# Graph convolution on one core: sums of moving node blocks pass through DRAM to 49 fixed blocks

## The chip, the cores and the metric

The kernel runs on one core of a Trainium2 chip. The metric is the device time of one execution in microseconds, the median of several runs. TensorE appears in the profile as PE (its weight loads as PEld), VectorE as DVE, ScalarE as ACT, GpSimd as POOL, and the queue that issues the plain DMAs as SP.

## The reference

There are N = 6250 nodes with D = 512 features in float32 and E = 100000 edges, sorted by their target `dst`. With h the rectified layer norm of x, and norm = -dinv[src] * dinv[dst], where dinv is one over the root of a node's count as a source:

```
prop(h) = segment_sum(h[src] * norm, dst)            # 6250 x 512
h  = relu(layernorm(x))
h1 = leaky(layer_norm(h @ W1_0 + prop(h) @ W1_1 + b1) * gamma + beta)
out = x + h1 @ W2_0 + prop(h1) @ W2_1 + b2
```

So each of two layers gathers 100000 rows of 2 KB by `src`, sums them by `dst`, and multiplies two 6250 x 512 matrices by two 512 x 512 weights.

## The kernel before

A setup of some 124 us loads x into the tile `places`, counts the sources, and makes `dinv`, the layer norm's scales and the table `tab[0]` of rows h * dinv that the first layer gathers. The second layer gathers from `tab[1]`, which the first layer writes, and reads its own rows back from `h_tab`.

The edges lie in 782 chunks of 128. `gather` (L400) is one indirect DMA on POOL: 128 rows of 2 KB into one of 57 slots of `places`, the slots being used in a ring. A gather waits until PE has done with the slot's earlier chunk.

The nodes are worked on in moving blocks. `block_plan` cuts the edges at every 1888th edge into BL = 53 blocks; block b starts at the node where edge 1888 b lies, read from `dst` at run time, so each block's edges lie in chunks that are known when the program is built, while its first node is known only at run time. On the mean a block owns 118 nodes and not 128, and its rows in x, h_tab, tab[1] and out are addressed through a register on SP (`row[b]`). 15 new chunks are needed by a block, and about 24 pairs of chunk and quarter of a block are multiplied.

PE, POOL and SP follow the order of the program, which is written by hand; ACT and DVE are ordered by the scheduler. For block b, in each layer, the program has:

- gathers up to 57 chunks past the block's first one (`gather_to`);
- `load(b + 2)`: SP loads `xt` (L474), and `scales` (L477, first layer) or `h` (L479, second layer);
- `own(b + 1)`: four transposes of h on PE (L460), copied to `hT` by ACT (L488);
- `sums(b)`: DVE compares edge targets with the block's nodes (`sel`, L507), PE multiplies `sel` into the gathered rows (L517, 32 columns of the array at a time, so four products at once), ACT copies the result to `agg`, scaled by the nodes' -dinv (L520);
- half of block b + 1's own products (`start_products`, L495, 4 PE instructions), four transposes of `agg` (L460), a copy to `aT` on DVE (L603), the other half of L495, and the products of `aT` with the other weight (L609, 8 PE instructions);
- `finish`: DVE and ACT do bias and layer norm (first layer) or bias and residual (second), and SP stores to `tab[1]` and `h_tab` (L546, L550) or to `out` (L529).

A count of the edges that were seen, and checks on the block starts, decide at the end whether a slow general path runs as well.

Of the kernel before, what the change touches and what calls it, by code (L numbers as in the profile page):

```python
# [19 lines left out]
P = 128  # L20
# [7 lines left out]
RAW = 60  # L28
SPREAD = 3.2
# [35 lines left out]
def gnn_kernel(  # L65
# [34 lines left out]

    nc = tc.nc
# [24 lines left out]
    scales = dram.tile([3, NB * P], F32, name="scales")  # L126

# [10 lines left out]
    signs = const.tile([P, 2], F32, name="signs")  # L138
# [6 lines left out]
    sb = const.tile([P, BL, 3], F32, name="sb")  # L145
    sn = const.tile([P, BL, 2], F32, name="sn")
# [84 lines left out]
    nc.gpsimd.memset(signs[:, 0:1], -1.0)  # L231
    nc.gpsimd.memset(signs[:, 1:2], SLOPE)
# [18 lines left out]
    all3 = ep.tile([P, 3, NB], F32, name="all3")  # L251
# [4 lines left out]
    for (i0, n), t in zip(groups, xs):  # L256
        n = min(n, NB - LAST - i0)
        for j in range(n):
            junk = ep.tile([P, D], BF, name="junk", bufs=2)
            nc.scalar.activation(junk, t[:, j, :], AF.Copy, accum_out=sums[:, i0 + j : i0 + j + 1])  # L260
        nc.scalar.activation(nm_all[:, i0 : i0 + n], sums[:, i0 : i0 + n], AF.Copy, scale=-1.0 / D)
        for j in range(n):
            junk = ep.tile([P, D], BF, name="junk", bufs=2)
            nc.scalar.activation(junk, t[:, j, :], AF.Square, bias=nm_all[:, i0 + j : i0 + j + 1],
                                 accum_out=sq_all[:, i0 + j : i0 + j + 1])
# [42 lines left out]
    with tc.tile_pool(name="fold", bufs=1) as dp, tc.tile_pool(  # L308
        name="fold_ps", bufs=1, space=bass.MemoryType.PSUM
    ) as dps:  # L310
        deg = dps.tile([P, NB], F32, name="deg")
        each = ident.rearrange("k (n s) -> k s n", s=2)
        for t in range(2):
            for i in range(2):
                nc.tensor.matmul(deg[t * LO : (t + 1) * LO, :], each[:, i, :], both[:, :, t, i],
                                 start=(i == 0), stop=(i == 1))
        root = dp.tile([P, NB], F32, name="root")
        some = dp.tile([P, NB], F32, name="some")
        nc.vector.tensor_scalar_max(root, deg, 1.0)
        nc.scalar.activation(root, root, AF.Sqrt)  # L320
        nc.vector.tensor_single_scalar(some, deg, 0.0, op=OP.is_gt)
        nc.vector.reciprocal(root, root)
        nc.vector.tensor_mul(dinv, root, some)
        nc.vector.tensor_scalar_mul(ndinv, dinv, -1.0)
        nc.vector.tensor_copy(all3[:, 2, :], dinv)

        nc.vector.tensor_mul(sc[:, 0, :], rs_all, dinv)
        nc.vector.tensor_mul(sc[:, 1, :], nb_all, dinv)
# [20 lines left out]
    odd = ep.tile([1, 2, BL], F32, name="odd")  # L349
# [10 lines left out]
    with tc.tile_pool(name="scales_ps", bufs=1, space=bass.MemoryType.PSUM) as fps:  # L360
        all_ps = fps.tile([NB, 3, P], F32, name="all_ps")
        for k in range(3):
            nc.tensor.transpose(all_ps[:, k, :], all3[:, k, :], ident)
        all_sb = ep.tile([NB, 3, P], F32, name="all_sb")
        nc.scalar.activation(all_sb, all_ps, AF.Copy)
        nc.sync.dma_start(scales.rearrange("k (b p) -> b k p", p=P), all_sb)

# [4 lines left out]
    n_unseen = nc.values_load(unseen[0:1, 0:1], min_val=0, max_val=2 * BL,  # L372
# [6 lines left out]
def usual_path(tc, have):  # L379
    nc = tc.nc  # L380
    (x, out, tab, h_tab, scales, sidx, dl, iota_r, w_sb, W2_1, W2_0, w_late, ident, eps, ones, first_i, first, owned,
     astray, signs, sb, sn, bias1, bias2, gam, bet, n_seen, unseen, ranges, NK, N, E, D, NB, BL, NC, KD, places,
     order, groups, xs, sc, pick, src_lo, src_hi, p_id) = (
        have[n] for n in ("x out tab h_tab scales sidx dl iota_r w_sb W2_1 W2_0 w_late ident eps ones first_i first "
                          "owned astray signs sb sn bias1 bias2 gam bet n_seen unseen ranges NK N E D NB BL NC KD "
                          "places order groups xs sc pick src_lo src_hi p_id").split())
    AHEAD = 2
    R = len(order)
    with ExitStack() as es:
# [3 lines left out]
        row = {}  # L393
# [24 lines left out]
        def find(tag, bufs):  # L418
# [7 lines left out]
            is_lo.append(pool.tile([P, 4, P], F32, name="is_lo"))  # L426
# [3 lines left out]
        def look_up(tag, bufs):  # L430
# [4 lines left out]
            at = looked  # L435
            assert at + 4 <= gathered
# [5 lines left out]
            nc.vector.tensor_tensor(is_hi, src_hi[:, at : at + 4, None].to_broadcast([P, 4, NB]),  # L442
# [6 lines left out]
            for j in range(4):  # L449
                nc.scalar.activation(zr(at + j), zr(at + j), AF.Relu, bias=ac[:, j, 1:2], scale=ac[:, j, 0:1])  # L450
# [13 lines left out]
        def load(layer, b):  # L464

            if b % LOADED == 0:
# [4 lines left out]
                for k in range(n):  # L471
                    row[b + k] = bass.ds(vals[k], P)
            xt = pool.tile([P, D], F32, name="xt", bufs=AHEAD + 1)
            nc.sync.dma_start(xt, x[row[b], :])  # L474
            h = pool.tile([P, D], F32, name="h", bufs=AHEAD + 1)
            if layer == 0:
                nc.sync.dma_start(sb[:, b, :], scales[:, row[b]].rearrange("k p -> p k"))  # L477
            else:
                nc.sync.dma_start(h, h_tab[row[b], :])  # L479
            return xt, h  # L480

        def own(layer, b, xt, h):

            if layer == 0:
                nc.vector.tensor_tensor(sn[:, b, :], sb[:, b, 2:3].to_broadcast([P, 2]), signs, op=OP.mult)
                nc.scalar.activation(h, xt, AF.Relu, bias=sb[:, b, 1:2], scale=sb[:, b, 0:1])
            ps, hT = transposed(h, "hT")
            nc.scalar.activation(hT, ps, AF.Copy)  # L488
            if layer == 1 and b == BL - 1:
                nc.vector.tensor_add(xt, xt, bias2)  # L490
            return hT

        def start_products(u_ps, hT, w0, kcs):
            for kc in kcs:
                nc.tensor.matmul(u_ps, hT[:, kc, :], w0[:, kc, :], start=(kc == 0), stop=False)  # L495

        def sums(layer, b):
            rng = ranges[b]
            at = [sum(hi - lo for lo, hi in rng[:q]) for q in range(NQ + 1)]
# [5 lines left out]
            for q, (lo, hi) in enumerate(rng):  # L505
                wide = [P, hi - lo, Q]
                nc.vector.tensor_tensor(sel[:, at[q] : at[q + 1], :], dl[:, lo:hi, None].to_broadcast(wide),  # L507
                                        node[:, None, q * Q : (q + 1) * Q].to_broadcast(wide), op=OP.is_equal)
            if layer == 0:
                held = pool.tile([P, NK, Q], BF, name="held", bufs=1)  # L510
                nc.scalar.activation(held[:, : at[NQ], :], sel[:, : at[NQ], :], AF.Copy,
                                     accum_out=n_seen[:, b : b + 1])
            ps = psum.tile([P, D], F32, name="ps")
            for s in range(max(hi - lo for lo, hi in rng)):
                for q, (lo, hi) in enumerate(rng):
                    if lo + s < hi:
                        nc.tensor.matmul(ps[q * Q : (q + 1) * Q, :], sel[:, at[q] + s, :], zr(lo + s),  # L517
                                         start=(s == 0), stop=(lo + s == hi - 1))
            agg = pool.tile([P, D], F32, name="agg", bufs=1)
            nc.scalar.activation(agg, ps, AF.Copy, scale=sn[:, b, 0:1])  # L520
            return agg

        def finish(layer, b, v, xt):
            if layer == 1:
                o = pool.tile([P, D], F32, name="t")
                if b < BL - 1:
                    nc.vector.tensor_add(v, v, bias2)  # L527
                nc.vector.tensor_add(o, v, xt)
                nc.sync.dma_start(out[row[b], :], o)  # L529
# [14 lines left out]
            nc.scalar.activation(t, v, AF.Copy, scale=sn[:, b, 1:2])  # L544
            nc.vector.scalar_tensor_tensor(t, v, sb[:, b, 2:3], t, op0=OP.mult, op1=OP.max)
            nc.sync.dma_start(tab[1][row[b], :], t)  # L546
# [3 lines left out]
            nc.sync.dma_start(h_tab[row[b], :], g)  # L550
# [6 lines left out]

        ACT = mybir.EngineType.Activation
# [3 lines left out]
        held = [load(0, b) for b in range(AHEAD)]  # L562
# [4 lines left out]
        for layer in range(2):  # L567
            w0, w1 = (w_late[:, 1], w_late[:, 0]) if layer else (w_sb[1], w_sb[0])
            if layer == 1:
                gathered = 0  # L570
                held = [load(layer, b) for b in range(AHEAD)]
            for b in range(BL):
# [7 lines left out]
                if b == 0:  # L580
                    hT = own(layer, 0, *held[0])
# [5 lines left out]
                if b + AHEAD < BL:  # L587
                    held.append(load(layer, b + AHEAD))
                if b + 1 < BL:
                    hT = own(layer, b + 1, *held[b + 1])  # L590
# [3 lines left out]
                agg = sums(layer, b)  # L594
# [4 lines left out]
                if b + 1 < BL:  # L599
                    next_ps = psum.tile([P, D], F32, name="u_ps")  # L600
                    start_products(next_ps, hT, w0, range(KD // 2))
                aT_ps, aT = transposed(agg, "aT")
                nc.vector.tensor_copy(aT, aT_ps)  # L603
                if b + 1 < BL:
                    start_products(next_ps, hT, w0, range(KD // 2, KD))
                if layer == 0:
                    another()
                for kc in range(KD):
                    nc.tensor.matmul(u_ps, aT[:, kc, :], w1[:, kc, :], start=False, stop=(kc == KD - 1))  # L609
# [5 lines left out]
                finish(layer, b, u_ps, held[b][0])  # L615
                u_ps = next_ps
# [329 lines left out]
```

## Time and profile before

| | |
|---|---|
| median of 7 runs | 2693.85 us (2684.55 to 2718.3) |
| the profiled execution | 2683.43 us, its span 2681.6 us |
| busy: PE, DVE, ACT, POOL | 71%, 25%, 18%, 56% of the span |
| DMA | 527.33 MB, mean 197 GB/s |
| gathers | 1504 of 0.95 us each, and 60 from x itself |
| first layer | from about 124 us to 1421 us of the span |
| second layer | from 1421 us to the end |

An instruction's row in the profile has its start, its duration and, in brackets, how long its engine had been idle before it and what ended that; "remote" stands for a release that the profile cannot put down to an instruction. Ends of PE's instructions are modelled.

### The profile page before, as it was taken

How to read it: one execution, taken by the hardware profiler on the slowest of the kernel's cores; microseconds unless marked ns; L12 is line 12 of the kernel's file. 1: busy time of each engine (PE TensorE's matmuls, PEld its weight loads, DVE VectorE, ACT ScalarE, POOL GpSimd, SP SyncE). 2: the span in 40 equal slices, each digit the busy share in tenths (PEclk: the TensorE clock that was granted, in tenths of full speed). 3: DMA queues.
4: the chain of work that ended last, by engine and by line, in shares of the span. 5: the costliest groups of instructions: out<-in, count | busy, mean ns of one | idle time of the engine just before them, and what ended most of it. 6: DMA issues, size and time to landing. Idle time of an engine off the chain costs nothing.

```text
span 2681.6 us, 23467 instructions
## 1 busy us (share of the span) xinstructions
PE 1906.7 (71%) x8137; PEld 731.6 (27%) x8137; DVE 681.8 (25%) x1422; ACT 471.7 (18%) x924; POOL 1502.8 (56%) x1579
## 2 busy tenths in 40 slices
PE   4627768777777876776683378777777677786878
PEld 4413223222222222222231123222222222222323
DVE  8923323322322332232240111111111111111111
ACT  8723212222211221121120000000000000000000
POOL 4254565666655665565516566655665565666560
PEclk9757889888988988888896688888988798897989
DMA  9474666767657765665626576766676666766672
GB/s 319 173 252 141 197 202 198 216 204 215 200 176 229 212 201 170 195 204 182 185 92 197 161 215 208 219 192 187 211 216 187 201 209 195 219 207 206 189 213 72
DMA packets 209696, 527.33 MB, mean 197 GB/s; under 512 B 51850, under 2 KB 53559, under 8 KB 209566
## 3 DMA queue, kind: packets, MB, share of 16 engines
q0 software_dynamic: 125120, 410.09, 52.2%
q1 hardware_dynamic: 84446, 115.63, 12.4%
q8 instruction: 66, 1.08, 0.2%
q14 instruction: 64, 0.52, 0.1%
HBM read 471.00 MB, written 54.60 MB: 196 GB/s over the span
## 4 chain that ended last, share of the span: by engine, by line
PE 40%; another core or an unknown queue 30%; issue 14%; DVE 11%; ACT 3%; DMA 0%; POOL 0%; SPq 0%; ACTq 0%; DVEq 0%; POOLq 0%
PE u_ps L609 17%; PE ps L517 15%; PE u_ps L495 6%; DVE sel L507 2%; DVE aT L603 1%; PE aT_ps L460 1%; PE hT_ps L460 1%; DVE lo L285 1%; DVE hi L285 1%; DVE g L549 1%; DVE u_ps L541 1%; DVE u_ps L539 1%; DVE node L504 1%; DVE u_ps L531 1%
## 5 line engine op out<-in xcount | busy, mean ns | idle before, releaser
L400 POOL DMA_INDIRECT places<-tab,sidx x1504 | 1426.9, 949 | 1029.0 <-PE ps L517 425.7
L517 PE MATMUL ps<-places,sel 128*32 128x512 f32 x4984 | 786.2, 620 | 129.3 <-issue 116.8
L517 PEld LDWEIGHTS ps<-places,sel 128*32 128x32 f32 x4984 | 197.8, 112 | 628.5 <-issue 607.0
L609 PE MATMUL u_ps<-places,aT 128*128 128x512 f32 x424 | 253.9, 754 | 141.1 <-DVE aT L603 114.7
L507 DVE TENSOR_TENSOR sel<-dl,node 128x192 f32<-128x192 f32 (+3 forms) x424 | 122.7, 346 | 777.0 <-remote 482.2
L495 PE MATMUL u_ps<-w,hT 128*128 128x512 f32 x424 | 244.4, 706 | 100.5 <-issue 87.8
L609 PE MATMUL u_ps<-w,aT 128*128 128x512 f32 x424 | 240.9, 721 | 94.5 <-DVE aT L603 89.8
L495 PE MATMUL u_ps<-places,hT 128*128 128x512 f32 x424 | 227.9, 663 | 7.5 <-issue 7.5
L488 ACT ACTIVATE hT<-hT_ps 128x512 f32<-128x512 f32 x106 | 63.2, 596 | 940.3 <-PE hT_ps L460 607.3
L520 ACT ACTIVATE agg<-ps,sn 128x512 f32<-128x512 f32 x106 | 72.9, 687 | 783.9 <-remote 463.9
L460 PE MATMUL aT_ps<-ident,agg 128*128 128x128 f32 x424 | 74.1, 302 | 153.4 <-ACT agg L520 85.3
L609 PEld LDWEIGHTS u_ps<-places,aT 128*128 128x128 f32 x424 | 100.0, 245 | 299.6 <-issue 155.1
L603 DVE COPY aT<-aT_ps 128x512 f32<-128x512 f32 x106 | 73.3, 692 | 425.5 <-remote 321.8
L609 PEld LDWEIGHTS u_ps<-w,aT 128*128 128x128 f32 x424 | 96.8, 234 | 230.3 <-issue 123.8
L495 PEld LDWEIGHTS u_ps<-w,hT 128*128 128x128 f32 x424 | 85.4, 224 | 216.6 <-issue 195.2
L460 PEld LDWEIGHTS aT_ps<-ident,agg 128*128 128x128 f32 x424 | 55.4, 156 | 236.9 <-issue 126.3
L527 DVE TENSOR_TENSOR u_ps<-u_ps,bias 128x512 f32<-128x512 f32 x52 | 36.4, 700 | 305.1 <-PE u_ps L609 153.0
L495 PEld LDWEIGHTS u_ps<-places,hT 128*128 128x128 f32 x424 | 78.8, 206 | 115.7 <-issue 115.7
L460 PE MATMUL hT_ps<-ident,h 128*128 128x128 f32 x424 | 65.8, 279 | 58.6 <-DVE is_lo L427 29.2
L531 DVE TENSOR_TENSOR u_ps<-u_ps,bias 128x512 f32<-128x512 f32 x53 | 37.1, 700 | 258.5 <-PE u_ps L609 171.1
L400 POOL DMA_INDIRECT places<-in_x_dram,sidx x44 | 44.1, 1003 | 81.1 <-ACT places L413 55.1
L460 PEld LDWEIGHTS hT_ps<-ident,h 128*128 128x128 f32 x424 | 53.7, 144 | 115.2 <-issue 90.5
(117 smaller groups left out, 986.7 us busy)
## 6 DMA issues: line engine op xcount, KB each, us to landing
xt<-in_x_dram SPq DMA_DIRECT2D x106, 256.0 KB
places<-tab,sidx POOLq DMA_INDIRECT x1504
tab<-t SPq DMA_DIRECT2D x53, 256.0 KB
h_tab<-g SPq DMA_DIRECT2D x53, 256.0 KB
h<-h_tab SPq DMA_DIRECT2D x53, 256.0 KB
out_dram<-t SPq DMA_DIRECT2D x53, 256.0 KB
places<-in_x_dram SPq DMA_DIRECT2D x4, 1792.0 KB
tab<-places SPq DMA_DIRECT2D x4, 1792.0 KB
```

The lines of the kernel that those rows point to most:

```text
L285: nc.vector.tensor_tensor(t, s[:, g * 2 * GJ : (g + 1) * 2 * GJ].rearrange("p (j s) -> p j s", s=2)[:, :, None, :] .to_broadcast([EP, GJ, ...
L400: nc.gpsimd.indirect_dma_start(out=zr(t), out_offset=None, in_=x if layer == 0 and t < RAW else tab[layer], in_offset=bass.IndirectOffsetO ...
L460: nc.tensor.transpose(ps[:, kc, :], h[:, kc * P : (kc + 1) * P], ident)
L488: nc.scalar.activation(hT, ps, AF.Copy)
L495: nc.tensor.matmul(u_ps, hT[:, kc, :], w0[:, kc, :], start=(kc == 0), stop=False)
L507: nc.vector.tensor_tensor(sel[:, at[q] : at[q + 1], :], dl[:, lo:hi, None].to_broadcast(wide), node[:, None, q * Q : (q + 1) * Q].to_broad ...
L517: nc.tensor.matmul(ps[q * Q : (q + 1) * Q, :], sel[:, at[q] + s, :], zr(lo + s), start=(s == 0), stop=(lo + s == hi - 1))
L520: nc.scalar.activation(agg, ps, AF.Copy, scale=sn[:, b, 0:1])
L527: nc.vector.tensor_add(v, v, bias2)
L531: nc.vector.tensor_add(v, v, bias1)
L603: nc.vector.tensor_copy(aT, aT_ps)
L609: nc.tensor.matmul(u_ps, aT[:, kc, :], w1[:, kc, :], start=False, stop=(kc == KD - 1))
```

## The change

The moving blocks stay for the sums alone. ACT copies block b's sums to `agg` unscaled, and SP writes them to a new DRAM table `sum_d` at the block's rows (register address). Behind that stand NB = 49 fixed blocks of 128 nodes (the last one starts at N - 128). `need[i]` is the moving block after which all rows of fixed block i are there, if block starts are off from their even spacing by at most `DRIFT` = 32 nodes, which a new term of the check tests. After the write of block need[i], SP reads rows of `sum_d` into `prop[i]`, and ACT scales them by `ndinv`. `dense(i)` then does what followed the sums before: own transposes, both products and `finish`, for fixed block i, one moving block later than its read. In each layer the moving blocks 0, 1, 10, 23, 36 and 49 (of 0 to 52) are followed by the next block's sums with no `dense` between; all others are followed by one `dense`, and before the sums of block 52 stand two more, of fixed blocks 46 and 47, whose rows block 51 completes. The last fixed block is the last moving block too, and takes its sums without DRAM.

Own rows (`h`, `xt`), `tab[1]`, `h_tab` and `out` have fixed addresses, and scales come from tiles of the setup, so the first layer's loads of `scales` go. `own(i + 1)` stood before `sums` and now stands in `dense`, after the sums. One more pass over the node rows' scales (`last3`) is read back in the setup.

```diff
         def sums(layer, b):
...
-            agg = pool.tile([P, D], F32, name="agg", bufs=1)
-            nc.scalar.activation(agg, ps, AF.Copy, scale=sn[:, b, 0:1])
-            return agg
+            agg = pool.tile([P, D], F32, name="agg")
+            if b == BL - 1:
+                nc.scalar.activation(agg, ps, AF.Copy, scale=last_nd)
+                prop[NB - 1] = agg
+                return
+            nc.scalar.activation(agg, ps, AF.Copy)
+            nc.sync.dma_start(sum_d[row(b), :], agg)
+            for i in range(NB):
+                if need[i] == b:
+                    prop[i] = pool.tile([P, D], F32, name="prop")
+                    nc.sync.dma_start(prop[i], sum_d[at[i] : at[i] + P, :])
+                    nc.scalar.activation(prop[i], prop[i], AF.Copy, scale=ndinv[:, i : i + 1])
...
+        def dense(layer, i, u_ps, w0, w1):
+            if layer == 1:
+                own_x[i] = pool.tile([P, D], F32, name="xt")
+                nc.sync.dma_start(own_x[i], x[at[i] : at[i] + P, :])
+                if i == NB - 1:
+                    nc.vector.tensor_add(own_x[i], own_x[i], bias2)
+            if i + AHEAD < NB:
+                load(layer, i + AHEAD)
+            next_ps = None
+            if i + 1 < NB:
+                hT = own(layer, i + 1)
+                next_ps = psum.tile([P, D], F32, name="u_ps")
+                start_products(next_ps, hT, w0, range(KD // 2))
+            aT_ps, aT = transposed(prop.pop(i), "aT")
+            nc.vector.tensor_copy(aT, aT_ps)
+            if i + 1 < NB:
+                start_products(next_ps, hT, w0, range(KD // 2, KD))
+            for kc in range(KD):
+                nc.tensor.matmul(u_ps, aT[:, kc, :], w1[:, kc, :], start=False, stop=(kc == KD - 1))
+            finish(layer, i, u_ps)
+            return next_ps
...
-                if b + AHEAD < BL:
-                    held.append(load(layer, b + AHEAD))
-                if b + 1 < BL:
-                    hT = own(layer, b + 1, *held[b + 1])
...
-                agg = sums(layer, b)
+                if b == BL - 1:
+                    while need[i] < b:
+                        u_ps = dense(layer, i, u_ps, w0, w1)
+                        i += 1
+                sums(layer, b)
...
+                while i < NB and need[i] < b + (b == BL - 1):
+                    u_ps = dense(layer, i, u_ps, w0, w1)
+                    i += 1
```

Counts for both layers together: sums 106 as before; `dense` passes 98 for 106; 104 writes of 256 KB to `sum_d` and 96 reads; 294 other block loads and stores of 256 KB for 318.

## The prediction

> **What bounds the kernel now.** I read the busy times first, then the list of waits, then the timeline of three stretches: the blocks at the very end, a block in the middle of the second layer, and that layer's start. The span of the profiled execution is 2681.6 us and its time 2683.4; the median of the runs is 2693.85, so I add 10.4 at the end. A difference of 0.5%, 13.5 us, is about what a measurement of this kernel can tell from none.
>
> ```profile
> PE 1906.7 (71%) x8137; PEld 731.6 (27%) x8137; DVE 681.8 (25%) x1422; ACT 471.7 (18%) x924; POOL 1502.8 (56%) x1579
> L400 POOL DMA_INDIRECT places<-tab,sidx x1504 | 1426.9, 949 | 1029.0 <-PE ps L517 425.7
> ```
>
> A gather takes 0.95 us and 0.30 to the next, so the 15 of a block take 18.75 us and the 782 of a layer 978 us. Between the sums of blocks 0 and 49 of the second layer (their `agg` at 1509.19 and 2627.01) lie 49 periods of 22.8 us. POOL is therefore not the bound by itself: it waits 425.7 us for PE to free slots.
>
> Now the waits on PE's results:
>
> ```profile
> ACT agg L520 <- remote: 463.9, 64, 74.1
> POOL places L400 <- PE ps L517: 425.7, 152, 15.0
> DVE aT L603 <- remote: 321.8, 49, 10.6
> PE u_ps L609 <- DVE aT L603: 204.5, 49, 6.9
> ```
>
> The two handoffs from PE that carry a block, `agg` and `aT`, are late in about half of the blocks without a releaser that the profile can name. The last two blocks of the program, whose gathers are all done, show the chain without this:
>
> ```profile
> 2640.07 1.98 PE L495 MATMUL u_ps<-places,hT 128*128 128x512 f32 x4
> 2640.25 0.69 ACT L520 ACTIVATE agg<-ps,sn 128x512 f32<-128x512 f32 x1 [5.55 <-PE ps L517]
> 2641.89 0.60 PE L460 MATMUL aT_ps<-ident,agg 128*128 128x128 f32 x4
> 2642.33 1.88 PE L495 MATMUL u_ps<-places,hT 128*128 128x512 f32 x4
> 2642.53 0.69 DVE L603 COPY aT<-aT_ps 128x512 f32<-128x512 f32 x1 [1.12 <-PE aT_ps L460]
> 2644.05 3.60 PE L609 MATMUL u_ps<-places,aT 128*128 128x512 f32 x8
> 2647.48 0.60 PE L460 MATMUL hT_ps<-ident,h 128*128 128x128 f32 x4
> 2648.01 6.21 PE L517 MATMUL ps<-places,sel 128*32 128x512 f32 x46
> ```
>
> From one `agg` (2640.25) to the next (2654.32) there are 14.07 us: 6.2 of sums and 7.9 of everything else on PE. PE never stands still, since half of L495 lies over each handoff. The block at 1900 us, with gathers going, looks different:
>
> ```profile
> 1900.79 0.69 ACT L520 ACTIVATE agg<-ps,sn 128x512 f32<-128x512 f32 x1 [7.71 <-remote]
> ...
> 1908.51 0.69 DVE L603 COPY aT<-aT_ps 128x512 f32<-128x512 f32 x1 [6.17 <-remote]
> ...
> 1909.25 5.83 PE L609 MATMUL u_ps<-places,aT 128*128 128x512 f32 x8 [5.35 <-DVE aT L603]
> ```
>
> The transposes for this `aT` stand at 1901.53 to 1902.19, the copy at 1908.51. PE has idled 5.35 us by then, and its next eight products take 5.83 us and not 3.60, at half the clock. Over all blocks `agg` begins 2.3 us after the last row of the sums (0.1 in the last four blocks) and `aT` 2.3 us late in the first layer and 3.6 in the second (0.04 without gathers). All long cases lie where POOL has issued gathers without a pause for some 7 us or more. The strongest case is the second layer's start, where 57 empty slots let POOL run without a pause:
>
> ```profile
> 1438.76 6.19 PE L517 MATMUL ps<-places,sel 128*32 128x512 f32 x34 [3.40 <-DMA places<-tab,sidx]
> ...
> 1496.57 0.95 POOL L400 DMA_INDIRECT places<-tab,sidx  x1 [0.30 <-issue]
> 1505.82 0.95 POOL L400 DMA_INDIRECT places<-tab,sidx  x1 [8.30 <-remote]
> 1509.19 0.69 ACT L520 ACTIVATE agg<-ps,sn 128x512 f32<-128x512 f32 x1 [74.13 <-remote]
> ```
>
> Sums that PE had by 1448 are handed over at 1509, after the run of gathers. So the bound is PE's chain of handoffs, stretched from 14.1 us a block to 22.8 by POOL's gathers.
>
> **The change, part by part**, on the profiled 2683.4 us.
>
> *Eight passes fewer* (four in each layer) of L495, L460, L609 and `finish`. Their cost at most is a period less its sums, 22.8 - 6.1 = 16.7 us each, 134 in all. At least it is nothing, for the gathers of those blocks remain. The nearest row is the layer's start: where PE frees many slots at once, POOL runs on end, and PE's handoffs stand until it ends. Two sums in a row free 30 slots, which is half of that run. So I credit what a period has beyond its own 15 gathers, 22.8 - 18.75 = 4.05 us each: **-32** (-134 to 0).
>
> *A hop moves behind the sums.* `own(i + 1)` stood before the sums, and ACT's copy of `hT` (0.60 us) lay beside them. Now PE transposes h behind the sums and stands until ACT has made `agg` (0.69, ahead of `hT` in ACT's order) and `hT`. Before, it went on at once with half of L495. Without gathers, the last sums to the end of the `aT` transposes takes 2642.49 - 2640.14 = 2.35 us. After: 0.1 to `agg`, 0.69, 0.04, 0.60 and 0.05 make 1.5, then half of L495 (1.72 without its overlap) and 0.6 for the transposes, 3.8. The transposes of h no longer stand ahead of the sums, 0.53. That is 3.8 - 2.35 - 0.53 = 0.95 for each of 96 passes: **+92** (0, if late handoffs cover it, to 92).
>
> *The late handoff loses its cover.* `agg` is late by over 1 us in 64 of 106 blocks, and 1.9 us of L495 stood over it. Only the 0.6 of the transposes do now, since ACT works `agg` off first, and `hT` stands behind it. All of that is 1.3 x 64 = 83, and for 98 passes in place of 106, 75. But a gather run ends when it ends, and a late `hT` makes `aT` less late. I take a third: **+25** (0 to 75).
>
> The clock enters here. After 5.35 us without work the eight of L609 took 5.83 us for 3.60; the new stop of 1.5 us is far from that. [...]
>
> *The way through DRAM.* SP writes `sum_d`, waits for the landing, reads `prop`, and ACT scales it (0.69). At the second layer's start POOL was released 2.92 us after the store to `tab[1]` was issued (1418.39 to 1421.31), and PE's transposes came 4.56 us after the issue of the load of h (1421.88 to 1426.44). The trip is then 0.69 + 2.9 + 4.6 + 0.69, about 9 us, against 22.8 to the pass that needs it. Where two sums stand on end, at four places of each layer, another 6.1 us of sums is the least cover: up to 3 us each, 23. ACT's scale stands in ACT's order ahead of `hT` and the next `agg`, so a late trip would stop these, and PE with them; SP's loads of h and `xt` queue behind the read, two blocks ahead of need. I take **0** (0 to 23). [...]
>
> *The layers' ends.* Pass 47 needs block 51, which pass 45, 46's products and the trip's 9 us overlap: **0** (0 to 18, both trips bare).
>
> *Scales.* In the first layer ACT waited 77.9 us in 24 pieces for loads of `scales`, which go. PE itself waited 9.9 us for ACT's `h`: **-10** (-78 to 0).
>
> *Bytes.* 104 writes and 96 reads of 256 KB less 24 loads: 46 MB on 527, 9%. At 197 GB/s that would be 234 us if the path were the bound; but gathers land 3.3 us after issue and are issued two blocks ahead, and PE waits 6.6 us for them in all. **0** (0 to 60, which is a quarter of that).
>
> *The rest.* Setup's extra read **+3**; 96 scales on ACT (18% busy), SP's issues and DVE's unchanged work 0, under the sums.
>
> Sum: -32 + 92 + 25 + 0 + 0 - 10 + 0 + 3 = +78; 2683.4 + 78 + 10.4 = **2772 us**.
>
> **The rivals.** *Fewer passes pay in full.* If the new hop falls into lateness that the gathers set anyway, and POOL's 33 tiles of lead carry the double sums, the gain is up to 134: -134 - 10 + 3, 2552 us; with 4 us a pass it is 2655. I put it at 2610. For it: 8 x 16.7 is the largest term here, and POOL waits on PE. Against it: the 57-gather run, where lead did not help. It decides if the hop costs under 1.4 us a pass (134 / 96). *Nothing moves*: gain and hop cancel, 2694. *The trip stands in the way*: `prop`'s wait holds ACT ahead of each `agg`. With a trip at 9 us it can't, but at over 22.8 it does; 2.5 us at each pass would be +240, about 2930. Against it: the 2.92 and 4.56 us rows, taken beside a busy DMA. *The general path runs*, if block starts drift by over 32 nodes: these edges drift by 18 at most, so it is nearly excluded.
>
> **How the numbers follow.** The forecast gets 0.59, full pay 0.25, no change 0.10, the trip 0.05, the general path 0.01. That makes faster 0.25, same 0.10, slower 0.65. The forecast's own range is 2710 to 2880: the hop half covered at one end, lateness uncovered and 40 us of bytes and trips at the other. Down to the other case's middle it is 2605 to 2880, with a tenth left out on either side.
>
> **What would show it.** In the profile after: PE's first half of the own products (now L496) waiting for ACT's `hT` behind each sums, about 1.5 us in the blocks without gathers, where `agg` to `agg` should be 15.0 for 14.07; about 23.7 with gathers; ACT's `agg` still released by "remote"; no waits on `scales`; about 573 MB; and next to no wait of the scaling of `prop` (L541) on DMA, but for the double sums. I am wrong if the period with gathers stays at or under 22.8 (then the hop is covered), if two sums in a row cost no longer run of late handoffs, or if L541 waits at most blocks.

## The result

The changed kernel takes 2867.99 us (median of 20 runs, 2845.34 to 2893.11) against 2696.5 of the kernel before (52 runs); the ratio is 1.0709, with an interval of 1.0677 to 1.0741. It is slower, as forecast, and inside the range, but the forecast of +78 us was less than half of it: 7.09% of 2693.85 are +191. Below, one hundredth of a ratio is taken as 27 us. Beside two of the runs below, e17 and m4, the kernel before itself took 2090.8 us, so these two are compared with that value alone.

The changed kernel's busy times and its gathers, from its page:

```profile
PE 1886.4 (66%) x7945; PEld 736.7 (26%) x7945; DVE 650.0 (23%) x1328; ACT 516.0 (18%) x996; POOL 1499.9 (53%) x1577
...
L414 POOL DMA_INDIRECT places<-tab,sidx x1504 | 1426.3, 948 | 1171.3 <-PE ps L528 579.5
```

PE has 192 products and transposes fewer and 20 us less work, and the span is 162 us longer. POOL's gathers cost what they did; POOL waits 154 us longer for PE to free slots (579.5 for 425.7). So PE stands more. Its list of waits (total, number, longest) says at what:

```profile
ACT agg L535 <- remote: 763.9, 57, 85.1
...
DVE aT L593 <- remote: 569.4, 53, 12.6
...
PE u_ps L496 <- ACT hT L491: 293.6, 61, 13.2
...
ACT prop L541 <- DMA prop<-sum_d: 242.7, 47, 10.1
...
PE u_ps L597 <- DVE aT L593: 183.1, 55, 6.5
```

The third line is new: the products of the own rows (L496, which was L495) wait for the copy `hT`. So is the fourth: ACT waits 47 times, 5.2 us on the mean, for the read of `sum_d`. One block of the second layer in the timeline (start, duration, idle time before and its releaser):

```profile
1915.13 0.66 PE L474 MATMUL hT_ps<-ident,h 128*128 128x128 f32 x4
...
1917.49 0.60 ACT L535 ACTIVATE agg<-ps 128x512 f32<-128x512 f32 x1 [15.43 <-remote]
...
1920.41 0.60 ACT L491 ACTIVATE hT<-hT_ps 128x512 f32<-128x512 f32 x1 [2.33 <-remote]
...
1921.07 3.78 PE L496 MATMUL u_ps<-places,hT 128*128 128x512 f32 x4 [5.27 <-ACT hT L491]
...
1930.93 0.69 DVE L593 COPY aT<-aT_ps 128x512 f32<-128x512 f32 x1 [11.87 <-remote]
1931.68 5.40 PE L597 MATMUL u_ps<-places,aT 128*128 128x512 f32 x8 [4.18 <-DVE aT L593]
```

The transposes of h end at 1915.79, and ACT copies them at 1920.41, although it was free from 1918.09. PE stands 5.27 us, and its next four products take 3.78 us where four took 1.98 without gathers; the granted clock is 0.50 over these 3.78 us, and 0.82 over the whole span (0.86 before). The handoff of `aT` is late all the same: the transposes of `prop` end at 1925.70, and DVE copies them at 1930.93. At the end of the layer, without gathers, the same place looks as it was priced:

```profile
2780.99 0.66 PE L474 MATMUL hT_ps<-ident,h 128*128 128x128 f32 x4
...
2782.33 0.58 ACT L491 ACTIVATE hT<-hT_ps 128x512 f32<-128x512 f32 x1
2782.96 1.98 PE L496 MATMUL u_ps<-places,hT 128*128 128x512 f32 x4 [1.31 <-ACT hT L491]
```

From the starts of the sums in both traces: a moving block of the second layer, blocks 3 to 50, takes 25.15 us for 22.78 before. As only 43 of these 47 have a pass, that is 27.5 a pass. The first layer's go from 23.59 to 23.76. From block 50 to the last sums the two layers take 70.7 and 55.6 us where they took 35.3 and 33.9.

### The profile page after: what moved, and what is told of

Same layout as the page of the kernel before. It is cut to its first block, busy times and chain, and to the rows that moved or that the text cites. A ratio compares the mean times of both kernels' runs of the same rounds, so it can differ in the third digit from the quotient of the medians.

```text
span 2843.4 us, 22620 instructions
## 1 busy us (share of the span) xinstructions
PE 1886.4 (66%) x7945; PEld 736.7 (26%) x7945; DVE 650.0 (23%) x1328; ACT 516.0 (18%) x996; POOL 1499.9 (53%) x1577
## 4 chain that ended last, share of the span: by engine, by line
another core or an unknown queue 34%; PE 32%; issue 15%; DVE 12%; DMA 3%; ACT 3%; SPq 1%; POOL 1%; ACTq 0%; DVEq 0%; POOLq 0%
PE u_ps L597 12%; PE ps L528 11%; PE u_ps L496 6%; DVE sel L518 2%; DVE aT L593 1%; DMA sum_d<-agg 1%; PE aT_ps L474 1%; PE hT_ps L474 1%; DMA prop<-sum_d 1%; DVE hi L287 1%; DVE t L548 1%; DVE node L515 1%; DVE g L569 1%; DVE st L554 1%
## 5 line engine op out<-in xcount | busy, mean ns | idle before, releaser
L414 POOL DMA_INDIRECT places<-tab,sidx x1504 | 1426.3, 948 | 1171.3 <-PE ps L528 579.5
L528 PE MATMUL ps<-places,sel 128*32 128x512 f32 x4984 | 746.2, 609 | 123.6 <-issue 100.6
L496 PE MATMUL u_ps<-w,hT 128*128 128x512 f32 x392 | 271.8, 831 | 253.1 <-ACT hT L491 141.7
L496 PE MATMUL u_ps<-places,hT 128*128 128x512 f32 x392 | 266.9, 818 | 241.7 <-ACT hT L491 151.9
L597 PE MATMUL u_ps<-places,aT 128*128 128x512 f32 x392 | 216.6, 704 | 120.6 <-DVE aT L593 113.9
L535 ACT ACTIVATE agg<-ps 128x512 f32<-128x512 f32 x104 | 62.1, 597 | 1157.4 <-remote 763.9
L597 PE MATMUL u_ps<-w,aT 128*128 128x512 f32 x392 | 203.0, 666 | 71.8 <-DVE aT L593 69.2
L496 PEld LDWEIGHTS u_ps<-w,hT 128*128 128x128 f32 x392 | 95.0, 269 | 343.0 <-issue 176.6
L496 PEld LDWEIGHTS u_ps<-places,hT 128*128 128x128 f32 x392 | 92.6, 262 | 327.9 <-issue 163.1
L541 ACT ACTIVATE prop<-prop,ndinv 128x512 f32<-128x512 f32 x96 | 69.2, 720 | 513.0 <-issue 270.4
L597 PEld LDWEIGHTS u_ps<-places,aT 128*128 128x128 f32 x392 | 84.9, 225 | 248.4 <-DVE aT L593 140.7
L597 PEld LDWEIGHTS u_ps<-w,aT 128*128 128x128 f32 x392 | 81.5, 214 | 188.4 <-issue 100.1
L474 PEld LDWEIGHTS aT_ps<-ident,prop 128*128 128x128 f32 x384 | 73.4, 202 | 96.3 <-issue 95.1
L474 PE MATMUL aT_ps<-ident,prop 128*128 128x128 f32 x384 | 85.0, 364 | 0.1
```

The costliest lines, as they stand in the source:

```text
L414: nc.gpsimd.indirect_dma_start(out=zr(t), out_offset=None, in_=x if layer == 0 and t < RAW else tab[layer], in_offset=bass.IndirectOffsetO ...
L474: nc.tensor.transpose(ps[:, kc, :], h[:, kc * P : (kc + 1) * P], ident)
L528: nc.tensor.matmul(ps[q * Q : (q + 1) * Q, :], sel[:, cols[q] + s, :], zr(lo + s), start=(s == 0), stop=(lo + s == hi - 1))
L535: nc.scalar.activation(agg, ps, AF.Copy)
L541: nc.scalar.activation(prop[i], prop[i], AF.Copy, scale=ndinv[:, i : i + 1])
```

## The experiments

**The hop, undone and alone.** e1 puts the own transposes of the next fixed block ahead of the sums again; e2 moves them behind the sums in the kernel before.

```diff
# e1, in the changed kernel
+                early = own(layer, i + 1) if b < BL - 1 and need[i] < b and i + 1 < NB else None
                 sums(layer, b)
...
-                hT = own(layer, i + 1)
+                hT = own(layer, i + 1) if hT is None else hT
...
# e2, in the kernel before
-                if b + 1 < BL:
-                    hT = own(layer, b + 1, *held[b + 1])
...
                 agg = sums(layer, b)
...
                 if b + 1 < BL:
+                    hT = own(layer, b + 1, *held[b + 1])
                     next_ps = psum.tile([P, D], F32, name="u_ps")
...
```

> The changed kernel with the own transposes of the next fixed block and ACT's hT put back ahead of the sums (where one pass follows the sums; the second pass of a pair keeps its own). Theory A, the hop: PE idles 5.0 us at each of 96 passes for a late hT, and half of what goes comes back as later aT; the time falls from 2868 to about 2650, below the kernel before, since eight passes of some 17 us are saved. Theory B, the way through DRAM (write, read, ACT's scaling ahead of the next copies) costs the time: within 40 us of 2868. Theory C, 46 MB more traffic: within 40 us of 2868.

> The kernel before with own(b + 1) moved behind the sums, nothing else. Theory A: the hop alone costs 2 to 3 us a block in the mean, 106 blocks: 2696 to about 2940. The price of the prediction (0.95 us a pass and 25 for lateness) gives about 2820. Theory B and C: within 30 us of 2696.

e1: 2710.21 us, 1.0074 of before (1.0014 to 1.0135), so the hop is worth 6.35 hundredths, 171 us, in the changed kernel. Theory A holds, but not its bonus: e1 is no faster than before. e2: 2822.33, 1.044 (1.0214 to 1.0666), which is 119 us; A's 240 was too much; the price on record, 117, fits the kernel before as far as four runs can tell (58 to 180 by the interval). In e1 the time that PE stood did not all go: it now stands at the next handoff.

```profile
1948.60 0.60 PE L474 MATMUL aT_ps<-ident,prop 128*128 128x128 f32 x4
...
1958.35 0.69 DVE L593 COPY aT<-aT_ps 128x512 f32<-128x512 f32 x1 [7.62 <-remote]
1959.10 5.46 PE L597 MATMUL u_ps<-places,aT 128*128 128x512 f32 x8 [8.18 <-DVE aT L593]
```

Ahead of L597 PE stands 264.8 us in e1's second layer, 5.4 for each of 49 passes; before, it stood 141.1 us ahead of L609, 2.7 for each of 53, with others ahead of the transposes.

**The way through DRAM.** e4 takes a scaled copy of block `need[i]`'s sums for `prop[i]`; e11 is e1 and e4 together.

```diff
-            nc.sync.dma_start(sum_d[row(b), :], agg)
             for i in range(NB):
                 if need[i] == b:
                     prop[i] = pool.tile([P, D], F32, name="prop")
-                    nc.sync.dma_start(prop[i], sum_d[at[i] : at[i] + P, :])
-                    nc.scalar.activation(prop[i], prop[i], AF.Copy, scale=ndinv[:, i : i + 1])
+                    nc.scalar.activation(prop[i], agg, AF.Copy, scale=ndinv[:, i : i + 1])
```

> The changed kernel without the way through DRAM: prop[i] is a scaled copy of the sums of block need[i], so the shift of rows between moving and fixed blocks is left out, and the write and read of sum_d with it. Theory A: only the exposed trips at the layers' ends and double sums go, 2868 to about 2800. Theory B: 2600 to 2650. Theory C: the traffic's share goes, up to 60 us: 2800 to 2840, not told from A by this run.

> e4 once more, beside the two that follow, since its interval (1.030 to 1.053 of before) and that of e10 (1.045 to 1.071) nearly touch. If the way through DRAM costs what e4 showed, 1.04 of before and 40 us or more under e10; if that was chance, within 20 us of e10.

> The two edits of e1 and e4 together: own transposes ahead of the sums, and prop[i] a scaled copy of the sums of block need[i] without the way through DRAM (the shift of rows is left out). If hop and trip are separate terms, 2868 - 158 - 61 = about 2650, some 45 below the kernel before, which is then what the saved passes and the scales bring. If the trip costs only through the hop (ACT's hT behind the scaling of prop), e11 equals e1, about 2710.

e4: 2806.5 us, 1.0417 (1.0301 to 1.0533), and once more 2784.77, 1.0242 (1.0165 to 1.0319): 79 and 126 us under the changed kernel. The two values of e4 lie 47 us apart for one and the same program, so a difference of that size between single results says little. e11: 2646.54, 0.9756 (0.9671 to 0.9841), 86 us under e1, between the other two differences: hop and DRAM are separate terms. What is left of the change without both is 66 us faster than before.

**Which part of it.** e10 is e4 with the write and the read put back, the read into a tile that nobody uses; e12 moves 32 of the 512 columns; e16 has the writes alone; in e17 ACT issues them, at fixed addresses.

```diff
# e10, in e4
+            nc.sync.dma_start(sum_d[row(b), :], agg)
             for i in range(NB):
                 if need[i] == b:
+                    unused = pool.tile([P, D], F32, name="unused")
+                    nc.sync.dma_start(unused, sum_d[at[i] : at[i] + P, :])
# e12, in e10: both cut to columns [: D // 16]
# e16: e10 without the read
# e17, in e16
-            nc.sync.dma_start(sum_d[row(b), :], agg)
+            nc.scalar.dma_start(sum_d[b * (step * N // E) : b * (step * N // E) + P, :] if b < 51 else sum_d[N - P : N, :], agg)
```

> e4 with the write to sum_d and the reads put back, but into a tile that nobody reads: the traffic of the changed kernel without a wait of ACT or PE for it (the shift of rows stays left out). If the wait for prop costs the 61 us: as e4, 2790 to 2820. If the 50 MB of traffic (or SP's part) do: as the changed kernel, 2850 to 2880.

> e10 once more beside e4 and e16: writes and reads of sum_d that nobody waits for. If they cost time, 1.06 of before; if not, as e4.

> e10 with each write to sum_d and each read cut to 32 of 512 columns: the same number of DMAs and of descriptors on SP's queue, a sixteenth of the bytes, nobody waiting. If the bytes cost the time: as e4, 2790 to 2820. If the DMAs' number, their descriptors or SP's waits for a landing do: as e10, 2860 to 2900.

> e4 with the writes of the sums to sum_d alone, without the reads, so SP waits for no landing of a write before its next loads (the shift of rows stays left out). If SP's wait for the landing delays the loads and stores behind it: as e4. If every DMA beside the gathers costs: half way from e4 to e10.

> e16 with the write of the sums issued by ACT right behind its copy, at addresses fixed when the program is built, so that SP neither waits for the copy nor reads an address register for it (the reads and the shift of rows stay left out). If the cost is SP's wait for the late copy, with loads and stores queued behind it, or the register: as e4, 1.024 to 1.042 of before. If it is the transfer beside the gathers: as e16, 1.054.

e10: 2892.95 us, 1.0582 (1.0451 to 1.0714), and again 2877.37, 1.0577 (1.051 to 1.0645). So some 1.3 hundredths, 35 us (about 15 to 55 by the intervals), of the change are a wait of ACT or PE for `prop`. e12: 2862.27, 1.0567 (1.0475 to 1.0658): a sixteenth of the bytes, in rows of 128 B, costs nearly as much, so it is not the number of bytes. e16, run beside e4_again and e10_again: 2861.62, 1.0538 (1.0473 to 1.0603). The write costs 80 us beside e4_again (1.0538 to 1.0242), but 33 against e4's first value (1.0417); the read with SP's wait for the write's landing costs 11, which is less than the intervals. e17 was to tell SP's queue from the transfer, but beside it the kernel before took 2090.8 us: 2139.02, 1.0232 (1.0218 to 1.0246), which answers nothing here. Why a write costs 0.3 to 0.8 us each (33 or 80 over 104) stays open. The traces don't place it either: 42 of the 56 us between e4_again and e16 (spans 2790.1 and 2846.1) lie in the first three blocks of the two layers, but in the trace of e4's first time the first layer's three took 136.3 us where e4_again's took 115.9. That SP's order does it is not excluded: in e16 SP stands 201.9 us in 27 pieces at the write until `agg` is there, with loads of h and xt behind it, and ACT's waits for the first layer's loads of h grow with the DMAs on SP:

```profile
ACT h L489 <- DMA h<-in_x_dram: 40.6, 18, 5.3
ACT h L489 <- DMA h<-in_x_dram: 65.9, 23, 6.7
ACT h L489 <- DMA h<-in_x_dram: 151.3, 24, 11.0
ACT h L489 <- DMA h<-in_x_dram: 168.3, 32, 8.3
```

These are e4_again, e16, e10_again and e12, in this order. What of them reaches PE no run tells.

**The passes.** e6 leaves out four passes of the second layer in the kernel before (`out` gets rows of x there).

```diff
...
+                left = [layer == 1 and c in (10, 23, 36, 49) for c in (b, b + 1)]
-                if b + 1 < BL:
+                if b + 1 < BL and not left[1]:
                     hT = own(layer, b + 1, *held[b + 1])
... (the pass's other parts stand under `not left[0]` or `not left[1]` in the same way)
-                finish(layer, b, u_ps, held[b][0])
+                if left[0]:
+                    nc.sync.dma_start(out[row[b], :], held[b][0])
+                else:
+                    finish(layer, b, u_ps, held[b][0])
```

> The kernel before with the dense pass of blocks 10, 23, 36 and 49 of the second layer left out (their own products, transposes, both weights' products and finish; out gets their rows of x). If a pass left out pays in full, 4 x 16.7 = 67 us less than before. By the price of the prediction, 4 x 4.05 = 16 us less. If the run of gathers behind two sums on end takes all of it back, no change.

2690.42 us, 0.9877 (0.9824 to 0.9931): 33 us less, 8.3 a pass (4.7 to 11.9): twice the 4.05 that was priced, and half of 16.7.

**No wait left on PE.** e3 is the changed kernel with the transposes of `prop` and h, and their copies, ahead of the sums; e13 puts the pass two blocks behind its read; e14 also loads h earlier. e5 does the like to the kernel before, without DRAM: the pass of block b - 1 stands behind the sums of block b.

```diff
# e3, in the changed kernel (e13: need[i] < b - 1, and always both; e14: load(layer, i + AHEAD) ahead of them)
+                if b < BL - 1 and need[i] < b:
+                    if had_dense:
+                        aT_ps, early_aT = transposed(prop.pop(i), "aT")
+                        nc.vector.tensor_copy(early_aT, aT_ps)
+                    if i + 1 < NB:
+                        early = own(layer, i + 1)
                 sums(layer, b)
...
# e5, in the kernel before (lines taken out are not shown)
...
+                if b:
+                    aT_ps, aT = transposed(agg, "aT")
+                    nc.vector.tensor_copy(aT, aT_ps)
+                    hT = own(layer, b, *held[b])
...
                 agg = sums(layer, b)
...
+                if b:
+                    next_ps = psum.tile([P, D], F32, name="u_ps")
+                    start_products(next_ps, hT, w0, range(KD))
...
+                    for kc in range(KD):
+                        nc.tensor.matmul(u_ps, aT[:, kc, :], w1[:, kc, :], start=False, stop=(kc == KD - 1))
...
+                    finish(layer, b - 1, u_ps, held[b - 1][0])
+                    u_ps = next_ps
+                if b + AHEAD < BL:
+                    held.append(load(layer, b + AHEAD))
... (the last block's pass follows its own sums)
```

> The changed kernel with both sets of transposes, of h and of prop, and their copies ahead of the sums (prop only where the block before had a pass). PE then waits for no copy behind the sums. Theory A1, PE's results are only signalled late while POOL gathers: both delays lie under the sums, the period falls from 27 to about 19 us, the pace of 15 gathers, and the time to 2350 to 2450. Theory A2, PE itself works slower while POOL gathers: delays come back in the sums, 2600 to 2700. Theory B: still above 2800.

> The changed kernel with the pass two moving blocks behind its read, and all transposes (of prop and h) ahead of the sums, so that neither a copy nor the way through DRAM is waited for. If PE's slow stretches under POOL's gathers are the bound and passes pay in full, 49 passes give 2520 (before with one block of lag) less 8 x 8 to 16 plus 61 for the traffic, 2450 to 2520. If the traffic costs more than the passes bring: 2520 to 2600.

> e13 with the load of the own rows, two passes ahead, issued before the transposes and not behind the sums. In e13 PE stood 4.5 to 5 us between the transposes of prop and those of h at 92 passes, for a load issued just before. If that wait was on the path: 2613 to about 2480, under the 2520 of e5. If PE's slow stretches take it up: 2580 to 2610.

> The kernel before, with the dense part of block b - 1 behind the sums of block b, and the transposes of agg and of h with their copies ahead of these sums: no DRAM, moving blocks, 53 passes. PE waits for no copy behind the sums, and agg has 7 us of products to be made in. Theory A1, results are only signalled late while POOL gathers: the period falls to the 19 us of 15 gathers, 2350 to 2450. Theory A2, PE itself works slower while POOL gathers: 2550 to 2650.

e3: 2620.29 us, 0.9743 (0.9622 to 0.9863); e13: 2613.01, 0.9653 (0.9563 to 0.9742), worse than expected, as PE then stood 4.5 to 5 us a pass for h; e14: 2551.09, 0.94 (0.933 to 0.947); e5: 2520.28, 0.9266 (0.9189 to 0.9342), the fastest that was run and faster than both kernels. Theory A1 falls with these. In e5's second layer PE stands at no handoff once the blocks run, and yet a block takes 21.45 us and not 19 or less: its sums spread out, 13.3 us on the mean where they take 6.2 without gathers and took 8.5 before. The clock is not the cause: the granted clock of its 100 us stretches from 1500 to 2400 us is 0.91 to 0.98. (In its first layer PE still stands some 140 us ahead of L495, and a block takes 21.48.)

```profile
1844.33 3.00 PE L517 MATMUL ps<-places,sel 128*32 128x512 f32 x17
...
1848.11 1.31 PE L517 MATMUL ps<-places,sel 128*32 128x512 f32 x2 [0.78 <-issue]
1850.23 4.97 PE L517 MATMUL ps<-places,sel 128*32 128x512 f32 x27 [0.81 <-issue]
...
1855.13 3.70 PE L495 MATMUL u_ps<-places,hT 128*128 128x512 f32 x8
...
1858.67 3.60 PE L606 MATMUL u_ps<-places,aT 128*128 128x512 f32 x8
```

So it is not only the signal that comes late under gathers in e5; PE itself gets on more slowly (13.3 us of sums for 6.2), with gaps ("issue", 201.8 us ahead of L517 in all, 116.8 before) in which it waits for nothing that the profile shows, and the wait appears where PE must hand over: ahead of L496 in the changed kernel, ahead of L597 in e1. The 49 passes of e14 do not undercut the 53 of e5.

**The gathers.** m2 replaces each by a plain DMA of 128 neighbouring rows on SP, m1 the same on POOL, m4 by an indirect DMA with a constant table of rising indices, all in the kernel before.

```diff
...
-            nc.gpsimd.indirect_dma_start(
-                out=zr(t), out_offset=None, in_=x if layer == 0 and t < RAW else tab[layer],
-                in_offset=bass.IndirectOffsetOnAxis(ap=sidx[:, t : t + 1], axis=0))
+            r0 = t * 8 % 48 * P
+            nc.gpsimd.dma_start(zr(t), (x if layer == 0 and t < RAW else tab[layer])[r0 : r0 + P, :])   # m2: nc.sync
...
# m4 (pidx is the constant table)
+                in_offset=bass.IndirectOffsetOnAxis(ap=pidx[:, t % 6 : t % 6 + 1], axis=0))
```

> The kernel before with each gather replaced by a plain DMA of 128 neighbouring rows of the same table, issued by SP: the choice of rows by index is left out, the bytes into the same slots stay. Theory P, POOL's issuing of indirect DMAs makes PE's results late: the lateness of agg and aT goes, the period falls to 14 to 16 us and the time to 1850 to 2000. Theory D, the DMA traffic into the slots does it: 2500 to 2700.

> As m2, but the plain DMA of 128 neighbouring rows is issued by POOL: the choice of rows by index is left out, POOL's issuing and the bytes stay. If it is POOL's issuing of DMAs that slows PE: lateness and time as in the kernel before if an issue takes as long, 2500 to 2700. If it is the indirection: near the 2042 of m2.

> As m1, the same neighbouring rows, but fetched by indirect DMAs with a constant table of rising indices (the choice of rows by edge is left out). If it is the indirect form that slows PE: near the kernel before, 2550 to 2720. If the scattered rows do: near the 1910 of m1.

m2: 2042.46 us, m1: 1909.81 (one run each, beside 2718.15 and 2729.53 of before). In both the lateness is gone. m1's DMA rate in 40 slices of the span and its gathers, from its page, and its waits at `agg` and `aT`:

```profile
GB/s 347 102 312 378 240 251 220 271 248 237 269 236 228 287 217 280 215 260 256 220 247 269 210 55 303 371 370 364 375 383 344 344 328 350 336 336 341 324 296 35
...
L401 POOL DMA_DIRECT2D places<-tab x1504 | 801.8, 536 | 883.6 <-PE ps L516 573.0
```

```profile
ACT agg L519 <- PE ps L516: 431.3, 105, 12.9
...
DVE aT L602 <- PE aT_ps L459: 105.2, 105, 7.5
```

The releasers are PE's own instructions, not "remote" (in m2's list too: 517.3 us in 105 waits for `agg`, 98.4 in 106 for `aT`), and a block of the second layer takes 13.86 us, near the 14.07 of the last blocks before, which have no gathers, while the DMA moves 324 to 383 GB/s in 13 slices of the span on end. So in these two runs neither the bytes into the slots nor POOL's issuing as such (0.54 us each) slows PE. m4 took 2089.87 us, beside 2090.8 of the kernel before: there indirect DMAs of the same form, 0.946 us each, made nothing late in m4's trace:

```profile
L403 POOL DMA_INDIRECT places<-tab,pidx x1504 | 1422.3, 946 | 477.0 <-issue 272.9
L520 PE MATMUL ps<-places,sel 128*32 128x512 f32 x4984 | 778.8, 669 | 236.7 <-DMA places<-tab,pidx 233.6
```

In m4's list of waits ACT's 104 for `agg` (736.9 us) and DVE's 105 for `aT` (111.4) end with PE's own instructions. PE waits for gathers, and for nothing else of note (28.3 us for h come next). The scattered rows make no difference there, and m4 doesn't tell the indirect form from the rows where the kernel before takes 2700 us. m1 and m2 changed both at once.

## Why the prediction went wrong

By its terms, in us, the measured ones from e1, e11 and the result (171 + 86 - 66 = 191):

| term | predicted | measured |
|---|---|---|
| hop behind the sums, with the late handoff's lost cover | +92 +25 | +171 (e1) |
| way through DRAM, bytes | 0, 0 | +86 (e11 against e1; 79 and 126 by e4) |
| passes, scales, ends and setup | -32 -10 +0 +3 | -66 (e11) |

The measured ones add up to 191 by the way they are taken. By their intervals each is good to some 20 to 30 us.

- **The direction and its main cause were right.** The hop alone outweighs the saved passes, PE waits for `hT`, and `agg` is still released by "remote". Without gathers the stop is 1.31 us, for 1.5 worked out; with gathers a block takes 23.76 and 25.15 us, for 23.7.
- **The step that failed: "The way through DRAM ... I take 0" and "Bytes ... 0".** Both looked for somebody who waits: the 9 us trip against 22.8 of cover, PE's wait for gathers. The runs show +86 (79 and 126 by e4), and most of it without a wait of ACT or PE for `prop`: e10's writes and reads, which nobody uses, cost all but some 35 us of it; the write costs more than the read (80 or 33 us for 11); e12's sixteenth of the bytes costs nearly the same (1.0567 of before for 1.0582). What in the write costs it stays open; that SP's loads "queue behind the read, two blocks ahead of need" was counted as nothing, and is the rival that no run settled. L541 also waited in 47 of 96 passes, against "next to no wait", though the trip itself was priced about rightly: in the block above write and read took 7.9 us from SP's issue to ACT's scaling (1918.11 to 1925.99), near the 7.5 of the two rows.
- **"The late handoff loses its cover ... I take a third: +25"** was mis-sized too. The 171 are just past the upper end of both rows together (92 + 75 = 167). The handoff of `hT` is late as `agg` was, PE stands 5.05 us ahead of L496 at the mean pass (495 us in 98 gaps), and in the block above the four products behind it took 3.78 us for 1.98. I had counted a stop of 1.5 us and so no loss of clock, which was my estimate, with no row of such a stop beside it. It was right without gathers, where four products took 1.98 us at a granted clock of 1.00 behind a stop of 1.31 (2782.96), and wrong with them, where four took 3.78 at 0.50 behind one of 5.27 (1921.07). In the kernel before, the eight behind 5.35 us ran at 0.50 for their first 4.25 us and at 0.63 over all 5.83, so not at half the clock throughout. The 784 products of L496 took 538.7 us where 848 of L495 had taken 472.3. In the kernel before the price fitted (119 by e2). In the first layer before, PE already stood some 1.9 us a block between the sums and L495 (100.5 us in all), which goes with that layer's blocks growing by 0.17 us only.
- **The passes** paid 8.3 us each by e6, twice the 4.05; but eight of these are not the whole of the last row, for the row *The layers' ends*, 0 (0 to 18), failed too. From block 50 to the last sums the changed kernel's trace has 57 us more, and e11's, without hop and DRAM, 51 more; two passes more stand there in each layer (44 to 47 against 50 and 51), some 13 us for each of the four by the 51. The starts and middles of e11's layers are 97 us shorter. Scales were not tried alone.
- **The rival of full pay** is excluded (the hop costs 171, 1.8 a pass and so over the 1.4 at which that case was to be decided; e6 is at half of 16.7), and so is that of the trip ahead of each `agg` (of its 240 us e10 leaves some 35). A point that I had not asked: whether PE's results are signalled late or made late. I priced the lateness as something that cover hides. e3, e5 and e14 show that hiding it gains only part; e5 shows the rest in the sums.
- **Slips in the working:** by its own terms the hop comes to 0.92 a pass and not 0.95, and in the trace 70 of the 106 `agg`, not 64, are over 1 us late (64 are over 2 us late). Neither moves the forecast by more than 5 us.

## What to carry to other kernels

In this kernel, where handoffs are late for no instruction's sake, a new handoff lasted 5.05 us on the mean, as long as a late one (5.35 in the block at 1900 us before), and not the 1.31 of the stretch without gathers. What it cost in the end was less, 171 us of 495, since other stops shrank (PE's idle time grew by 182 us in all); a run with the handoff undone tells. Transfers whose data nobody waits for cost 45 and 90 us here (e10 against e4, two pairs), and a sixteenth of their bytes cost nearly as much (1.0567 of before for 1.0582), so a term of zero for such transfers needs a wide bound. With sums, transposes and products on one engine, putting the products one block behind and all transposes ahead of the sums took 7% off this kernel without any DRAM.

## What the runs showed of the hardware

- In e5 PE gets on more slowly while POOL gathers with indirect DMAs of 128 rows of 2 KB: sums that take 6.2 us without gathers spread to 13.3. With plain DMAs of the same size, of neighbouring rows, on POOL (m1, 0.54 us an issue, up to 383 GB/s) or SP (m2) the waits for `agg` and `aT` in the lists end with PE's own instructions; one run each. Whether the indirect form or the scattered rows do it no run tells.
- This is not always so. Beside m4 and e17 the kernel before took 2090.8 us (9 runs, 2086.98 to 2093.91), 23% less than beside all others, and the traces of m4 and e17 show no "remote" handoffs of that kind: there a block of the second layer takes 18.4 and 18.3 us, near the 18.75 of 15 gathers. What differed no run tells. The record gives chip 1 for these as for e6, e12, e13 and m1, beside which the kernel before took 2729.53 us; and the gathers' packets took nearly as long, 0.17 us in m4 for 0.18 before, by the pages' shares. In e17 the stop for `hT` was 1.1 us on the mean.
- In this kernel 104 writes of 256 KB to DRAM beside the gathers cost 80 us of the total in one comparison and 33 in another (e16). Writes and reads of 16 KB each (e12, 1.0567 of before) cost nearly what those of 256 KB did (e10, 1.0582).
